# Two-layer graph attention on one core: layer 0's larger units scored and summed in two parts

## The chip, the cores and the metric

The kernel runs on one core of a Trainium2 chip. The metric is device time in microseconds from launch to end; lower is better. The engines are TensorE (PE, with its weight loads PEld), VectorE (DVE), ScalarE (ACT), GpSimd (POOL) and SyncE (SP); each works through its own queue in order and waits on semaphores for the others.

## The reference

Two graph attention layers over 8 batches of 2048 nodes with 256 channels, one adjacency matrix for all, each with a residual and a layer norm. Cut to layer 0, which the change touches:

```python
h1, h2, h3 = inp @ W1, inp @ W2, inp @ W3                 # per batch, 2048 x 256
e = leaky_relu(einsum('bnd,bmd->bnm', h1, h2), 0.2)
e = where(adj > 0, e, -1e12)
attention = softmax(e, axis=-1)
x = layernorm(x + relu(einsum('bnm,bmd->bnd', attention, h3)))
```

Layer 1 has four heads of 64 channels, logits that are sums of a source and a destination term, the same mask and softmax, elu, residual and layer norm. About one in 128 entries of adj is set, and the diagonal, so a node has some tens of neighbours at most.

## The kernel before

**Tiling.** The nodes are ranked by degree (in the setup) and cut into 16 tiles of 128 nodes. Tile t is given `SLOTS[t]` neighbour slots: 36, 24, 22, 21, 20, 19, 19, 18, 17, 17, 16, 15, 15, 14, 13, 12. A unit is one tile in one layer for one half h of the batches (four batches, `HB`). In layer 0 the units of half 0 run from t = 15 to t = 0, then those of half 1 in the same order; then 32 units of layer 1 follow. There are 298 slots in a half, so 596 in each layer.

**Gathering.** For each slot, POOL issues one indirect DMA (L196) that fetches, for each of the 128 nodes, the row of its k-th neighbour: 4 batches x 256 floats. Rows lie in `ring`, 16 buffers (`RING`) of two slots (`CHUNK`), 32 slots in all. A buffer is held from its gather until its last sum. In half 0 the neighbour lists of later tiles are made beside this (`neighbours`, L506 to L515), and their rows pass through the same ring.

**Scoring (`logits0`, DVE).** The product W1 W2^T is folded into the query: `u.g` (made in `before0` by transposing the tile's own rows and two projections). A slot takes four instructions (L568), one for each batch: a product of 128x256 with its sum as `e[:, b, k]`. When all slots of a part are scored, the softmax follows on a tile of 128 x 4 x K: leaky ReLU (L581), the mask's addition (L582), maximum (L586), subtraction (L587), exp on ACT (L588), sum (L591), reciprocal (L593) and scaling (L594).

**Summing (`sums0`).** For each slot ACT makes four diagonal matrices (L665, tile `dg`, four buffers, each of one slot) from the probabilities, and PE multiplies them with the slot's rows into two PSUM tiles of 128x512 (`acc`, L645, four buffers). The cut into 64x64 pieces spreads node halves over both tiles.

**After (`after0`).** The finished sums are copied to `hs` by ACT (L680), transposed on PE, projected with W3 (L427), and DVE adds the residual with the ReLU in it (L705) and takes the statistics (L384). ACT computes the inverse root from them (tile `z`, L395 and L396), normalises (L407), and PE transposes the result and makes layer 1's table rows (L729), which ACT copies (L737) and POOL stores.

**Parts.** A unit of more than 24 slots is scored and summed in two parts, each with a softmax of its own. That is t = 0 alone (18 + 18). At its end `shares` (L600 to L629) finds the common maximum of both parts, rescales, moves the factors to the nodes' places with eight PE records (L620) and two copies (L628); then ACT scales the first part (L686) and DVE adds the scaled second part (L689).

**Order.** The program is written out by a loop of ticks. Each tick belongs to one summed slot of the current unit. It issues gathers while ring buffers are free (`pump`), lets the scoring stream go on by up to two slots while `ahead`, the slots scored but not yet summed, is below a limit, and takes a step or two of the queues `starts` (`before0`), `ends` (`after0`) and `lists`. The limit is

```python
tick(left + units[min(j + 1, len(units) - 1)].K + LEAD)      # LEAD = 5
```

with `left` the slots of the unit still to be summed. A slot is scored at the earliest three ticks after its gather. POOL's instructions keep this order (`manual_schedule` for POOL); those of PE, DVE and ACT are ordered by the compiler, which takes the written order as priority.

Of the kernel before, what the change touches and what calls it, by code (L numbers as in the profile page):

```python
# [11 lines left out]
F32 = mybir.dt.float32  # L12
# [4 lines left out]
AF = mybir.ActivationFunctionType  # L17
ALU = mybir.AluOpType
# [18 lines left out]
SLOTS = (36, 24, 22, 21, 20, 19, 19, 18, 17, 17, 16, 15, 15, 14, 13, 12)  # L37
CHUNK = 2
RING = 16
LEAD = 5  # L40
LATE = 6

# [87 lines left out]
def fast_path(  # L130
# [27 lines left out]
    KC = C // P  # L158
    HB = B // 2
    HC = HB * C  # L160
    HG = HB * H
    HW = HC // 2
    CD = C + H
# [274 lines left out]
    class Unit:  # L438
        def __init__(self, layer, h, t):
            self.layer, self.h, self.t = layer, h, t  # L440
            self.K = SLOTS[t]
            self.name = f"{layer}_{h}_{t}"

            n = self.K if self.K <= RING * CHUNK * 3 // 4 else -(-self.K // 2)
            self.parts = [(k, min(n, self.K - k)) for k in range(0, self.K, n)]
            self.chunks = [[] for _ in self.parts]
            self.p = [None] * len(self.parts)
            self.ps = [None] * len(self.parts)

            self.m, self.s = [], []  # L450
            self.xo = None
            self.ready = False
# [99 lines left out]
    def logits0(u):  # L552

        while not u.ready:
            yield 0
        for i, (k0, K) in enumerate(u.parts):
            n, o = f"{u.name}_{i}", offs[u.t] + k0
            e = ep.tile([P, HB, K], F32, tag="e", name=f"e_{n}")
            for k in range(K):
                c, s = divmod(k, CHUNK)  # L560
                while len(u.chunks[i]) <= c:
                    yield 0
                while clock[0] < u.chunks[i][c][2] + 3:
                    yield 0
                rows = u.chunks[i][c][0]
                for b in range(HB):
                    jt = sp.tile([P, C], BF16, tag="j", name=f"j_{n}_{k}_{b}", bufs=4)
                    nc.vector.tensor_tensor_reduce(  # L568
                        out=jt,
                        in0=rows[:, s, ts(b, C)],  # L570
                        in1=u.g[:, ts(b, C)],
                        scale=1.0,
                        scalar=0.0,
                        op0=ALU.mult,
                        op1=ALU.add,
                        accum_out=e[:, b, k : k + 1],
                    )
                yield 1
            p = e
            wide = [P, HB, K]  # L580
            nc.vector.scalar_tensor_tensor(p, e, ALPHA, e, ALU.mult, ALU.max)  # L581
            nc.vector.tensor_tensor(  # L582
                p, p, neg[:, o : o + K].unsqueeze(1).to_broadcast(wide), ALU.add
            )
            m = sp.tile([P, HG], F32, tag="m1", name=f"m_{n}")[:, :HB]
            nc.vector.tensor_reduce(m, p, AX.X, ALU.max)  # L586
            nc.vector.tensor_tensor(p, p, m.unsqueeze(2).to_broadcast(wide), ALU.subtract)  # L587
            nc.scalar.activation(p, p, AF.Exp)  # L588
            yield 0
            sm = sp.tile([P, HG], F32, tag="s1", name=f"s_{n}")[:, :HB]  # L590
            nc.vector.tensor_reduce(sm, p, AX.X, ALU.add)  # L591
            if len(u.parts) == 1:
                nc.vector.reciprocal(sm, sm)  # L593
                nc.vector.tensor_tensor(p, p, sm.unsqueeze(2).to_broadcast(wide), ALU.mult)  # L594
            u.m.append(m)
            u.s.append(sm)
            u.p[i] = p
            yield 0

    def shares(u, G):  # L600


        f = sp.tile([P, 2, HG], F32, tag="f", name=f"f_{u.name}", bufs=1)[:, :, :G]
        top = sp.tile([P, HG], F32, tag="top", name=f"top_{u.name}", bufs=1)[:, :G]
        nc.vector.tensor_tensor(top, u.m[0], u.m[1], ALU.max)
        for i in range(2):
            nc.vector.tensor_tensor(f[:, i, :], u.m[i], top, ALU.subtract)
        nc.scalar.activation(f, f, AF.Exp)
        for i in range(2):
            nc.vector.tensor_tensor(u.s[i], u.s[i], f[:, i, :], ALU.mult)  # L610
        nc.vector.tensor_tensor(top, u.s[0], u.s[1], ALU.add)
        nc.vector.reciprocal(top, top)
        nc.vector.tensor_tensor(f, f, top.unsqueeze(1).to_broadcast([P, 2, G]), ALU.mult)
        fs = sp.tile([P, 2, 2, HG // 2], F32, tag="fs", name=f"fs_{u.name}", bufs=1)
        fs = fs[:, :, :, : G // 2]
        for r in range(2):
            rr = slice(64 * r, 64 * r + 64)
            pf = ps_tile(f"ps_f_{u.name}_{r}")[:, :G].rearrange("p (i g) -> p i g", i=2)
            for c in range(2):
                nc.tensor.matmul(  # L620
                    pf[64 * c : 64 * c + 64],
                    lhsT=ident[rr, rr],
                    rhs=f[rr, :, ts(c, G // 2)],
                    start=True,
                    stop=True,
                    tile_position=(64 * r, 64 * c),
                )
            nc.vector.tensor_copy(fs[:, :, r, :], pf)  # L628
        return fs  # L629
# [23 lines left out]

    def sums0(u):
        accs = []
        for i, (k0, K) in enumerate(u.parts):
            while u.p[i] is None:
                yield 0
            acc = [acc_tile(f"acc_{u.name}_{i}_{r}") for r in range(2)]
            for k in range(K):  # L660
                c, s = divmod(k, CHUNK)
                rows, n, _ = u.chunks[i][c]
                diag = dp.tile([P, HB, 64], F32, tag="dg", name=f"dg_{u.name}_{i}_{k}")
                for b in range(HB):
                    nc.scalar.activation(  # L665
                        diag[:, b, :], twice, AF.Copy, scale=u.p[i][:, b, k : k + 1]
                    )
                while evictions:
                    evictions.popleft()()
                add_slot(acc, k, K, rows[:, s, :], diag)  # L670
                if s == n - 1:
                    credits[0] += 1
                yield 1
            accs.append(acc)

        def evict():
            u.hs = hsp.tile([P, HC], F32, tag="hs", name=f"hs_{u.name}")
            if len(accs) == 1:
                for r in range(2):
                    nc.scalar.copy(u.hs[:, ts(r, HW)], accs[0][r])  # L680
                return
            fs = shares(u, HB)
            for r in range(2):
                for j in range(2):
                    v = u.hs[:, ts(2 * r + j, C)]
                    nc.scalar.activation(  # L686
                        v, accs[0][r][:, ts(j, C)], AF.Copy, scale=fs[:, 0, r, j : j + 1]
                    )
                    nc.vector.scalar_tensor_tensor(  # L689
                        v, accs[1][r][:, ts(j, C)], fs[:, 1, r, j : j + 1], v, ALU.mult, ALU.add  # L690
                    )

        evictions.append(evict)

# [266 lines left out]
    def tick(limit):  # L961
        pump()
        while late and late[0][0] <= clock[0]:
            late.popleft()[1]()
        for _ in range(2):
            if ahead[0] < limit:
                ahead[0] += next(stream, 0)
        for queue in queues:
            for _ in range(min(len(queue), 2)):
                if queue and next(queue[0], queue) is queue:  # L970
                    queue.popleft()
        clock[0] += 1
# [5 lines left out]
    for j, u in enumerate(units):  # L978
        begun = False
        if 0 < j and j + 2 < NT:  # L980
            lists.append(neighbours(up[j + 2]))
        if j == NT:
            ends.append(checks())
        while len(ends) > 1:
            tick(0)
        if 2 <= j < 10:
            b, i = divmod(j - 2, 2)
            n = ts(i, N // 2)

            nc.gpsimd.dma_start(xg[1][n, ts(b, C)], x[HB + b, n])  # L990
        if j + 3 < 2 * NT:

            own_rows(units[j + 3])
        left = float(u.K)
        for share in sums[u.layer](u):
            ahead[0] -= share
            left -= share
            tick(left + units[min(j + 1, len(units) - 1)].K + LEAD)
            if not begun and left <= u.K / 2 and j + 3 < len(units):
                begun = True  # L1000
                v = units[j + 3]
                starts.append(before[v.layer](v))
        ends.append(finish(u))
# [300 lines left out]
```

## Time and profile before

| | |
|---|---|
| time, median of 11 runs | 2482.49 us (2478.58 to 2498.56) |
| the profiled execution | 2483.11 us, its span 2481.3 us |
| mean granted TensorE clock | 0.868 |
| layer 0, first to last accumulating matmul | 150 to 1482 us |
| L568, scores, DVE | 2384 instructions, mean 421 ns |
| L665, diagonals, ACT | 2384 instructions, mean 339 ns |
| L645, layer 0's sums, PE | 9536 records, mean 410 ns |
| L196, layer 0's gathers, POOL | 596, mean 1052 ns |

In the profile, "idle before" is an engine's idle time just ahead of an instruction, and the arrow names what ended it. In a list of waits, the columns are the total in us, how often, and the longest. Scores are pipelined on DVE: one takes 421 ns, but they start some 345 ns apart.

### The profile page before, as it was taken

How to read it: one execution, taken by the hardware profiler on the slowest of the kernel's cores; microseconds unless marked ns; L12 is line 12 of the kernel's file. 1: busy time of each engine (PE TensorE's matmuls, PEld its weight loads, DVE VectorE, ACT ScalarE, POOL GpSimd, SP SyncE). 2: the span in 40 equal slices, each digit the busy share in tenths (PEclk: the TensorE clock that was granted, in tenths of full speed). 3: DMA queues.
4: the chain of work that ended last, by engine and by line, in shares of the span. 5: the costliest groups of instructions: out<-in, count | busy, mean ns of one | idle time of the engine just before them, and what ended most of it. 6: DMA issues, size and time to landing. Idle time of an engine off the chain costs nothing. (4 is left out here: it accounts for less than half of the span.)

```text
span 2481.3 us, 52177 instructions
## 1 busy us (share of the span) xinstructions
PE 1790.9 (72%) x16675; PEld 968.9 (39%) x16675; DVE 2004.3 (81%) x7073; ACT 1430.6 (58%) x4849; POOL 1518.8 (61%) x1486
## 2 busy tenths in 40 slices
PE   1157888788889778889898888666556667755664
PEld 0134556455555555656555543222212122222221
DVE  6699688888888666777878856988888798888996
ACT  6244566666666656767666674643455466543545
POOL 3374455565666445655556565777677777775773
PEclk9678989898989899999999998788778888886887
DMA  9797778798886668888888777997899999977992
GB/s 382 265 350 257 287 275 325 272 323 294 291 295 235 205 231 274 288 277 302 302 272 304 257 266 266 342 355 270 314 351 353 344 352 359 347 275 292 349 352 97
DMA packets 249419, 734.92 MB, mean 296 GB/s; under 512 B 63200, under 2 KB 72544, under 8 KB 246704
## 3 DMA queue, kind: packets, MB, share of 16 engines
q0 software_dynamic: 192512, 645.89, 72.8%
q1 hardware_dynamic: 55360, 84.44, 10.0%
q8 instruction: 135, 2.21, 0.4%
q10 hardware_dynamic: 1264, 1.18, 0.2%
q14 instruction: 148, 1.21, 0.1%
HBM read 708.35 MB, written 76.09 MB: 316 GB/s over the span
## 5 line engine op out<-in xcount | busy, mean ns | idle before, releaser
L568 DVE CUSTOM_DVE_ANT_0 j<-s,g 128x256 bf16<-128x256 f32 x2384 | 855.5, 421 | 209.7 <-DMA s<-xg,idx 199.5
L196 POOL DMA_INDIRECT s<-xg,idx x596 | 626.7, 1052 | 517.5 <-PE acc L645 302.1
L645 PE MATMUL acc<-s,ident 64*64 64x512 f32 x4768 | 611.3, 665 | 348.0 <-issue 293.3
L645 PE MATMUL acc<-s,dg 64*64 64x256 f32 x9536 | 696.8, 410 | 150.6 <-ACT dg L665 139.8
L196 POOL DMA_INDIRECT s<-qg,idx x596 | 606.0, 1017 | 234.7 <-issue 130.4
L665 ACT ACTIVATE dg<-twice,e 128x64 f32<-128x64 f32 x2384 | 616.7, 339 | 91.2 <-PE acc L645 88.2
L846 DVE TENSOR_TENSOR s<-s,p 128x2048 f32<-128x2048 f32 (+1 forms) x260 | 574.8, 2233 | 0.0
L645 PEld LDWEIGHTS acc<-s,dg 64*64 64x64 f32 x9536 | 375.4, 141 | 413.7 <-ACT dg L665 228.8
L645 PEld LDWEIGHTS acc<-s,ident 64*64 64x64 f32 x4768 | 211.0, 150 | 740.1 <-issue 592.6
L842 ACT ACTIVATE s<-s,e 128x64 f32<-128x64 f32 x1408 | 342.7, 334 | 45.7 <-DVE e L810 37.7
L395 ACT ACTIVATE z<-st,roots 128x4 f32<-128x4 f32 x64 | 19.1, 298 | 368.8 <-DVE st L384 368.8
L568 DVE DVE_READ_ACCUMULATOR2_ANT e<- 128x1 f32 x2384 | 195.2, 82 | 0.0
L204 POOL DMA_INDIRECT out_dram<-o,oidx x128 | 128.6, 1005 | 67.7 <-ACT o L407 31.6
L780 DVE TENSOR_TENSOR e<-s,own 128x32 f32<-128x32 f32 (+1 forms) x306 | 56.7, 189 | 123.2 <-DMA s<-qg,idx 121.6
L729 PE MATMUL ps_q<-wqs,x1T 128*128 128x264 f32 x512 | 136.9, 404 | 7.3 <-ACT x1T L419 4.8
L427 PE MATMUL ps_p_g<-A,xT 128*128 128x256 f32 x512 | 130.5, 400 | 3.3 <-ACT xT L419 3.3
L427 PE MATMUL ps_p_h<-w_sb,hT 128*128 128x256 f32 x512 | 128.8, 395 | 2.5 <-ACT hT L419 2.5
L729 PEld LDWEIGHTS ps_q<-wqs,x1T 128*128 128x128 f32 x512 | 97.0, 197 | 36.0 <-ACT x1T L419 7.5
L407 ACT ACTIVATE o<-xr,nmr,rstd 128x256 f32<-128x256 f32 x128 | 66.5, 589 | 76.2 <-DVE nmr L403 69.5
L427 PEld LDWEIGHTS ps_p_g<-A,xT 128*128 128x128 f32 x512 | 96.8, 197 | 33.5 <-ACT xT L419 8.8
L427 PEld LDWEIGHTS ps_p_h<-w_sb,hT 128*128 128x128 f32 x512 | 93.6, 192 | 38.2 <-issue 13.6
L588 ACT ACTIVATE e<-e 128x72 f32<-128x72 f32 (+11 forms) x34 | 8.8, 259 | 135.5 <-DVE e L587 135.3
(138 smaller groups left out, 1479.5 us busy)
## 6 DMA issues: line engine op xcount, KB each, us to landing
adj<-in_adj_dram SPq DMA_DIRECT2D x16, 1024.0 KB
xr<-xo SPq DMA_DIRECT2D x128, 128.0 KB
x1s<-y SPq DMA_DIRECT2D x32, 512.0 KB
xr<-x1s SPq DMA_DIRECT2D x32, 512.0 KB
s<-xg,idx POOLq DMA_INDIRECT x596
s<-qg,idx POOLq DMA_INDIRECT x596
edges<-adj SPq DMA_DIRECT2D x16, 512.0 KB
xg<-in_x_dram SPq DMA_DIRECT2D x4, 2048.0 KB
```

What stands on the lines that cost most here:

```text
L196: nc.gpsimd.indirect_dma_start(out=dst, out_offset=None, in_=table, in_offset=AT(ap=index, axis=0), bounds_check=table.shape[0] - 1, oob_i ...
L204: ins = nc.gpsimd.indirect_dma_start(out=table, out_offset=AT(ap=index, axis=0), in_=src, in_offset=None)
L395: nc.scalar.activation(z, var, AF.Ln, bias=w.roots[:, 0:1], scale=1.0 / C)
L407: nc.scalar.activation(dst[:, b, :], y[:, b, :], AF.Identity, bias=nmr[:, b : b + 1], scale=rstd[:, b : b + 1],)
L427: nc.tensor.matmul(pp[:, ts(j, C)], lhsT=srcT[:, ts((2 * i + j) * KC + k, P)], rhs=weight[:, k, :], start=(k == 0), stop=(k == KC - 1),)
L568: nc.vector.tensor_tensor_reduce(out=jt, in0=rows[:, s, ts(b, C)], in1=u.g[:, ts(b, C)], scale=1.0, scalar=0.0, op0=ALU.mult, op1=ALU.add, ...
L645: nc.tensor.matmul(out, lhsT=lhsT, rhs=rhs, start=(k == 0 and j == 0), stop=(k == K - 1 and (j == 1 or diag is None)), tile_position=(64 * ...
L665: nc.scalar.activation(diag[:, b, :], twice, AF.Copy, scale=u.p[i][:, b, k : k + 1])
L729: nc.tensor.matmul(pq[:, : C + 2 * H], lhsT=x1T[:, ts(i * KC + k, P)], rhs=w.sqs[:, k, j * H : j * H + CD + H], start=(k == 0), stop=(k == ...
L780: nc.vector.tensor_tensor(e[:, c * CHUNK : c * CHUNK + ns, :].rearrange("p s (b g) -> p s b g", b=HB), rows[:, :ns, :].rearrange("p s (b w ...
L842: nc.scalar.activation(v[:, a, g, :], v[:, a, g, :], AF.Copy, scale=pv[:, a, g : g + 1])
L846: nc.vector.tensor_tensor(v, v, pv.unsqueeze(3).to_broadcast([P, n * HB, H, D]), ALU.mult)
```

## The change

- Units of layer 0 with 16 slots or more (t = 0 to 10, in both halves) are cut in two parts. The first part has an even number of slots: 24 = 12 + 12, 22 = 12 + 10, 21 = 10 + 11, 20 = 10 + 10, 19 = 10 + 9, 18 = 10 + 8, 17 = 8 + 9, 16 = 8 + 8; 36 stays 18 + 18. Units of layer 1 are cut as before.
- Both parts lie in one score tile, `both`. The second part's softmax runs over one more column that holds the first part's maximum. After the exp this column is the factor by which the first part's weights shrink; multiplied with the first part's sum it goes into the common sum. The second part is fully normalised, and the same column, normalised, is the first part's factor.
- `spread_shares` moves this factor to the nodes' places (PE, then two ACT copies) as soon as the second softmax is done.
- At the fourth slot of the second part's sums ACT writes the scaled first part to `hs`; when the second part is summed, DVE adds it. `shares` remains for layer 1.
- The limit for scoring ahead counts parts in place of units: what is left of the part, the next part, and 5.
- The mask's addition is an operation of its own, as it was.

```diff
+SPLIT = 16
@@ Unit
-            n = self.K if self.K <= RING * CHUNK * 3 // 4 else -(-self.K // 2)
-            self.parts = [(k, min(n, self.K - k)) for k in range(0, self.K, n)]
+            n = self.K
+            if layer == 0 and n >= SPLIT:
+                n = CHUNK * ((n + 2) // (2 * CHUNK))
+            elif n > RING * CHUNK * 3 // 4:
+                n = -(-n // 2)
+            self.parts = [(0, n), (n, self.K - n)][: 1 if n == self.K else 2]
@@ logits0
-            e = ep.tile([P, HB, K], F32, tag="e", name=f"e_{n}")
+            last = i == len(u.parts) - 1
+            if i == 0:
+                both = ep.tile([P, 2, HB, MOST], F32, tag="e", name=f"e_{n}")
+            e = both[:, i, :, : 1 + K + 1]
...
+            v = p
+            if i:
+                v = e[:, :, : 1 + K]
+                nc.vector.tensor_copy(e[:, :, 0], u.m[0])
...
+            if i:
+                v = e[:, :, 1:]
+                nc.vector.tensor_tensor(e[:, :, 1 + K], e[:, :, 0], u.s[0], ALU.mult)
+            nc.vector.tensor_reduce(sm, v, AX.X, ALU.add)
+            if last:
                 nc.vector.reciprocal(sm, sm)
...
+                if i:
+                    u.fs = spread_shares(u, e)
...
+    def spread_shares(u, e):
+        fs = sp.tile([P, 2, 2], F32, tag="f0", name=f"f0_{u.name}", bufs=2)
+        for r in range(2):
+            rr = slice(64 * r, 64 * r + 64)
+            pf = ps_tile(f"ps_f0_{u.name}_{r}")[:, :2]
+            for c in range(2):
+                nc.tensor.matmul(
+                    pf[64 * c : 64 * c + 64],
+                    lhsT=ident[rr, rr],
+                    rhs=e[rr, ts(c, 2), 0],
+                    start=True,
+                    stop=True,
+                    tile_position=(64 * r, 64 * c),
+                )
+            nc.scalar.copy(fs[:, r, :], pf)
+        return fs
@@ sums0
+                if i == 1 and k == 3:
+                    u.hs = hsp.tile([P, HC], F32, tag="hs", name=f"hs_{u.name}")
+                    for r in range(2):
+                        for j in range(2):
+                            nc.scalar.activation(
+                                u.hs[:, ts(2 * r + j, C)], accs[0][r][:, ts(j, C)], AF.Copy,
+                                scale=u.fs[:, r, j : j + 1],
+                            )
...
         def evict():
+            if split:
+                for r in range(2):
+                    v = u.hs[:, ts(r, HW)]
+                    nc.vector.tensor_tensor(v, v, accs[1][r], ALU.add)
+                return
@@ the tick loop
+        ends_of = [u.K - k0 - K for k0, K in u.parts]
+        follow = [K for _, K in u.parts[1:]] + [units[min(j + 1, len(units) - 1)].parts[0][1]]
...
-            tick(left + units[min(j + 1, len(units) - 1)].K + LEAD)
+            i = next(i for i, end in enumerate(ends_of) if left > end or end == 0)
+            tick(left - ends_of[i] + follow[i] + LEAD)
```

More of the change, by code (lines that the diff above doesn't have):

```diff
@@ L160, in fast_path @@
     HC = HB * C
+    MOST = 2 + max(SPLIT - 1, SLOTS[0] // 2)
     HG = HB * H
@@ L575, in logits0 @@
                         op1=ALU.add,
-                        accum_out=e[:, b, k : k + 1],
+                        accum_out=e[:, b, 1 + k : 2 + k],
                     )
                 yield 1
-            p = e
-            wide = [P, HB, K]
-            nc.vector.scalar_tensor_tensor(p, e, ALPHA, e, ALU.mult, ALU.max)
+            p = e[:, :, 1 : 1 + K]
+            nc.vector.scalar_tensor_tensor(p, p, ALPHA, p, ALU.mult, ALU.max)
             nc.vector.tensor_tensor(
-                p, p, neg[:, o : o + K].unsqueeze(1).to_broadcast(wide), ALU.add
+                p, p, neg[:, o : o + K].unsqueeze(1).to_broadcast([P, HB, K]), ALU.add
             )
+            v = p
+            if i:
+                v = e[:, :, : 1 + K]
+                nc.vector.tensor_copy(e[:, :, 0], u.m[0])
             m = sp.tile([P, HG], F32, tag="m1", name=f"m_{n}")[:, :HB]
-            nc.vector.tensor_reduce(m, p, AX.X, ALU.max)
-            nc.vector.tensor_tensor(p, p, m.unsqueeze(2).to_broadcast(wide), ALU.subtract)
-            nc.scalar.activation(p, p, AF.Exp)
+            nc.vector.tensor_reduce(m, v, AX.X, ALU.max)
+            nc.vector.tensor_tensor(
+                v, v, m.unsqueeze(2).to_broadcast([P, HB, v.shape[2]]), ALU.subtract
+            )
+            nc.scalar.activation(v, v, AF.Exp)
             yield 0
             sm = sp.tile([P, HG], F32, tag="s1", name=f"s_{n}")[:, :HB]
-            nc.vector.tensor_reduce(sm, p, AX.X, ALU.add)
-            if len(u.parts) == 1:
-                nc.vector.reciprocal(sm, sm)
-                nc.vector.tensor_tensor(p, p, sm.unsqueeze(2).to_broadcast(wide), ALU.mult)
+            v = p
+            if i:
[3 more added lines that the diff above has]
+            if last:
+                nc.vector.reciprocal(sm, sm)
+                v = p if i == 0 else e[:, :, : 1 + K]
+                nc.vector.tensor_tensor(
+                    v, v, sm.unsqueeze(2).to_broadcast([P, HB, v.shape[2]]), ALU.mult
+                )
+                if i:
+                    u.fs = spread_shares(u, e)
             u.m.append(m)
@@ L598, in logits0 @@
             yield 0
+    def spread_shares(u, e):
[11 more added lines that the diff above has]
+                    tile_position=(64 * r, 64 * c),
+                )
+            nc.scalar.copy(fs[:, r, :], pf)
+        return fs
     def shares(u, G):
@@ L655, in sums0 @@
         accs = []
+        split = len(u.parts) == 2
         for i, (k0, K) in enumerate(u.parts):
@@ L672, in sums0 @@
                     credits[0] += 1
+                if i == 1 and k == 3:
[5 more added lines that the diff above has]
+                                scale=u.fs[:, r, j : j + 1],
+                            )
                 yield 1
@@ L676, in evict @@
         def evict():
-            u.hs = hsp.tile([P, HC], F32, tag="hs", name=f"hs_{u.name}")
[L678 to L682, printed above, removed]
-            for r in range(2):
[L684 to L691, printed above, removed]
+            if split:
[3 more added lines that the diff above has]
+                return
+            u.hs = hsp.tile([P, HC], F32, tag="hs", name=f"hs_{u.name}")
+            for r in range(2):
+                nc.scalar.copy(u.hs[:, ts(r, HW)], accs[0][r])
         evictions.append(evict)
```

## The prediction, made before the changed kernel was run

> **What bounds the kernel now.** I read the busy totals first, then busy time by stretch, then the waits of each stretch, then the timeline of one unit, then the groups by shape.
>
> ```profile
> PE 1790.9 (72%) x16675; PEld 968.9 (39%) x16675; DVE 2004.3 (81%) x7073; ACT 1430.6 (58%) x4849; POOL 1518.8 (61%) x1486
> ```
>
> No engine is full over the span, so one has to go by stage. Layer 0 sums its slots from 150 to 1482 us. Two stretches of it hold the units that the change splits anew, t = 10 to 2, nine in each half (bounds: the ends of the units' last accumulating matmuls). Columns: busy time (and instructions) of PE, PEld, DVE, ACT, POOL, then granted clock, DMA share and GB/s.
>
> ```profile
> 334.80:720.50 385.70, 329.53 (x3392) 216.01 (x3392) 326.46 (x1778) 249.59 (x875) 220.40 (x211) 0.92 0.86 301
> 1016.70:1375.70 359.00, 323.70 (x3366) 209.08 (x3364) 280.77 (x1496) 246.56 (x862) 203.76 (x197) 0.96 0.86 294
> ```
>
> Call them A (half 0, neighbour lists are still being made on DVE) and B (half 1). PE is idle 56.2 us in A and 35.3 in B; DVE 59.2 and 78.2. PE is the fuller one, nearly level with DVE in A. Who is PE waiting for? First A, then B:
>
> ```profile
> ACT z L395 <- DVE st L384: 65.1, 9, 10.9
> POOL s L196 <- PE acc L645: 56.5, 29, 7.0
> PE acc L645 <- ACT dg L665: 54.8, 14, 7.1
> DVE j L568 <- DMA s<-xg,idx: 50.2, 37, 4.8
> ```
>
> ```profile
> POOL s L196 <- PE acc L645: 104.7, 58, 5.9
> DVE j L568 <- DMA s<-xg,idx: 70.3, 48, 5.1
> ACT z L395 <- DVE st L384: 44.0, 9, 7.2
> PE acc L645 <- ACT dg L665: 34.1, 15, 5.2
> ```
>
> Nearly all of PE's idle time (54.8 of 56.2; 34.1 of 35.3) ends with a diagonal from ACT, and ACT sits nine times in nine units at z, waiting for statistics from DVE. One unit of A, ACT and then PE:
>
> ```profile
> 429.01 1.06 ACT L665 ACTIVATE dg<-twice,e 128x64 f32<-128x64 f32 x4 [1.79 <-PE acc L645]
> 440.95 0.30 ACT L395 ACTIVATE z<-st,roots 128x4 f32<-128x4 f32 x1 [10.88 <-DVE st L384]
> ```
>
> ```profile
> 430.73 3.68 PE L645 MATMUL acc<-s,dg 64*64 64x256 f32 x64
> 441.55 5.20 PE L645 MATMUL acc<-s,dg 64*64 64x256 f32 x48 [7.13 <-ACT dg L665]
> ```
>
> ACT stands 10.88 us at z, so no diagonals are made; PE uses up those it has and then stands 7.13 us. So it is a ring of waits: DVE's statistics lie in its queue behind scored slots; those wait for landings (DVE's only large wait); the gathers wait for PE to free ring buffers; PE waits for ACT, ACT for DVE. PE never waits for a softmax itself: in these units the last score of a unit, counted off in the trace, ends 10 to 29 us before its first sum.
>
> **The change, part by part.** Mask: before adds it by an operation of its own too (L582), so this part is worth nothing.
>
> *Order.* This is the part with the gain. Counted in the trace of before, 33 to 36 slots past the unit's end are scored before its second statistics, in all eighteen units, and diagonals for 8 to 10 slots are made before z. The tick loop followed on paper gives nearly the same (31 to 36; 10 or 11), since the ring of 32 slots is the limit there, not `left + next K + 5`. With the new limit, `rest of the part + next part + 5`, the loop on paper puts 23 to 29 slots there: about 9 fewer. A slot costs DVE four scores started 0.345 us apart (the timeline), 1.38 us; nine are 12.4 us, more than any wait at z. So stretches could close up to the busier engine plus what is added.
>
> *DVE, per newly split unit.* Small operations take 0.16 us on 4 elements (L397) and about 0.23 on 72; at 40 elements I take 0.19. Unsplit, 18 slots: seven operations, 1.54 us. Split: 5 x 0.19, then 5 x 0.19 + copy 0.16 + product 0.16 + reciprocal 0.17 + last product 0.19, together 2.58: 1.0 more (0.8 to 1.2 with 0.16 or 0.23 for each). Eviction moves from ACT to DVE: two 128x512 additions reading PSUM, nearest row L892, 0.686 us: 1.37. Sum 2.4 us, for 20 units 48 us. It lies in DVE's idle 59.2 (A) and 78.2 (B); without that cover it is the slow rival below.
>
> *ACT.* Rows:
>
> ```profile
> L680 ACT COPY hs<-acc 128x512 f32<-128x512 f32 x60 | 31.8, 584 | 6.1 <-PE acc L645 6.1
> L686 ACT ACTIVATE hs<-acc,fs 128x256 f32<-128x256 f32 x8 | 3.1, 475 | 4.2 <-DVE fs L628 4.2
> ```
>
> Minus two copies (1.17), plus four scalings (1.90), one more exp (0.26), two tiny copies from PSUM (not in the trace; between nothing beyond their neighbour and 0.38 like L737; taken 0.29 like L396, 0.58 together): +1.6 us a unit. ACT is idle 136 us in A, 112 in B; covered, unless it falls where PE lives on its four diagonals.
>
> *PE.* Eight more matmul records of two columns a unit; L620's eight fill about 0.4 us with their weight loads: 9 us for 22 units, added to PE's floor.
>
> *New waits.* DVE is now waited for at three more places in a unit: transposes of hs (T) behind its eviction, PE's share matmuls behind the second softmax, ACT's second exp. Behind the share matmuls in PE's queue stand the following sums; behind ACT's share copies the next diagonals. Priced at the share matmuls: from the unit's end DVE has eviction 1.37, four slots 5.5, softmax 2.6, together 9.5 us; PE has till there four slots at 1.09, two transposes at 0.66 and a projection of 2.0, 7.7 us: 1.8 us of idle, and 0 if the compiler places them later (DVE, ACT and PE orders are its choice, only POOL's is kept as written: in the trace statistics stand up to 2.5 slots off the source's order in A and B, and 13 off at the last unit of half 0). I take 1.0 x 20 = 20 us; ends 0 and 36 us. The single hs buffer, now taken at slot 3 of part 1, was read out in the first slots of part 0, and the sums of part 0 are long done then: nothing. POOL issues the same gathers in the same order; the first part is even, so chunks stay as many.
>
> *The 36-slot units.* They were split already. Of the waits, PE stood 9.87 us at 836.48 and 4.63 at 1486.58 behind L686, which waited for L628 at the end of a chain of small DVE operations. Shares are now ready early and only the addition is left: 14.5 less about 4.5, a gain of 10.
>
> *Layer 1.* Its parts stay, its limit changes only beside the 36-slot unit, where the ring binds first: 0.
>
> **The sum.** A can fall to DVE's 326.5 + 9 x 2.4 = 348, a gain of at most 37.6; B to PE's 323.7 + 9 x 0.4 = 327, at most 31.7; the t = 11 units (idle 5.1 and 4.2, lead falls from 33 to 21) 9. t = 1 keeps its lead of 36 on paper: 0. Together 78, of which I take 60%, 47, because a DVE with idle time will be given later slots and drift back towards the ring's end. So 47 + 10 - 20 = 37 off. The profiled execution took 2483.11 us (span 2481.3 and 1.8 around it), 0.6 above the median of 11: 2446.
>
> A rule that speaks against this: Trainium skill, Perfetto Trace Analysis, Optimizing Scalar/DVE Operations, gives each DVE operation a fixed part, about 60 ns on SBUF and 125 on PSUM against ScalarE's 51 on PSUM, and advises larger operations on a saturated engine. By it (an estimate, with 1.03 ns an element from the rows above) seven more small operations and two PSUM additions of 512 cost 1.7 us a unit, 35 us in all, instead of the rows' 48, and the forecast would not move, for the cover is larger than both. The rows agree with its direction: L680 0.584 on ACT, L892 0.686 on DVE.
>
> **Rivals.**
>
> *DVE pays (slower), 0.34.* Place: A above all, where 50.2 of DVE's 59.2 idle us are landings: busy plus ring wait is the whole time. If the compiler fills DVE with later slots up to the ring's end, statistics stand behind 33 slots as before, and 2.4 us a unit go on top: 48, less 10 for the 36-slot units: 2521. It decides if the landing wait stays above some 5.5 us a unit in A. For: those 13 slots. Against: in A hardly any DVE time is free to be filled.
>
> *Handed back (no change), 0.14.* PE's wait at z goes, but share matmuls, eviction and second exp take it: 47 + 10 against 20 x 2.8: 2482.
>
> *Everything closes up, 0.10.* 78 + 10 off, no new wait: 2395. Against: PE and DVE would both have to run almost without a gap.
>
> **Numbers.** Forecast 0.42, 2446, its own range 2415 to 2472. What can be told from no change is about 0.3% (7.5 us). Faster: 0.42 + 0.10 and a little of the third, 0.53; within 0.3%: 0.12; slower: 0.35. The range for 8 in 10 reaches from 2405, where only the tail of "closes up" is left out, to 2505, half way up the slow case.
>
> **What would show it.** Right: z's wait for statistics in A and B falls from 109.1 us to below 50, landing waits fall from 120.5 with it, PE's idle time per unit falls to 2 to 4 us, no PE wait near 9.87 after the first 36-slot unit. Wrong: statistics still stand behind 33 scored slots; or PE waits for the share matmuls' DVE operations or for DVE's addition by more than 2 us a unit; or A's DVE shows the same landing waits and more busy time.

## The result and the profile after

The changed kernel takes 2592.26 us (median of 8 runs, 2583.7 to 2597.48), the kernel before 2485.24 beside it: a ratio of 1.0427, interval [1.0408, 1.0446]. It is 107 us slower where 37 us faster was forecast, outside the range. All of it lies in layer 0: its last sum ends at 1587.8 us in place of 1481.9, and what follows takes 991.8 in place of 999.5.

The page's busy totals of the changed kernel, then busy time in the same nine units of each half (A and B, cut at the ends of the same units' last sums, so the stretches are longer now):

```profile
PE 1812.4 (70%) x16835; PEld 974.7 (38%) x16835; DVE 2041.9 (79%) x7237; ACT 1445.4 (56%) x4951; POOL 1518.3 (59%) x1486
```

```profile
333.90:760.50 426.60, 341.70 (x3446) 214.75 (x3444) 340.47 (x1845) 253.43 (x912) 219.69 (x212) 0.91 0.79 273
1066.80:1474.00 407.20, 337.36 (x3438) 212.82 (x3442) 299.29 (x1583) 257.34 (x923) 205.14 (x196) 0.93 0.76 260
```

A is 40.9 us longer than before (426.6 to 385.7), B 48.2 (407.2 to 359.0). PE's idle time (stretch less its busy time) went from 56.2 to 84.9 and from 35.3 to 69.8. The waits of A, then of B:

```profile
POOL s L199 <- PE acc L687: 100.5, 32, 7.2
DVE j L578 <- DMA s<-xg,idx: 72.6, 49, 4.7
ACT e L603 <- DVE e L600: 69.7, 15, 9.5
PE ps_t_h L420 <- DVE hs L731: 52.3, 8, 10.1
...
PE acc L687 <- ACT dg L708: 21.2, 20, 3.4
...
ACT z L398 <- DVE st L387: 18.0, 8, 4.6
```

```profile
POOL s L199 <- PE acc L687: 134.6, 43, 9.1
DVE j L578 <- DMA s<-xg,idx: 95.5, 60, 4.0
ACT e L603 <- DVE e L600: 58.4, 15, 8.5
...
PE ps_t_h L420 <- DVE hs L731: 28.1, 6, 6.2
...
PE acc L687 <- ACT dg L708: 22.2, 21, 3.3
ACT z L398 <- DVE st L387: 21.4, 9, 4.5
```

The waits that the prediction named did fall: ACT at z from 109.1 us to 39.4, PE at the diagonals from 88.9 to 43.4. (Below 50 at z was the prediction's sign of being right. It is no sign of a gain: ACT's wait at the exps, the second one among them, rose from 48.3 us to 128.1 in A and B.) PE now stands at the transposes of hs, for DVE's addition of the two parts (L731), and DVE waits more for landings, 168.1 us in place of 120.5. One such place in A, PE first, then DVE:

```profile
657.42 1.96 PE L687 MATMUL acc<-s,dg 64*64 64x256 f32 x32
669.43 1.11 PE L420 MATMUL ps_t_h<-ident,hs 128*128 128x128 f32 x4 [10.06 <-DVE hs L731]
```

```profile
660.91 0.43 DVE L578 CUSTOM_DVE_ANT_0 j<-s,g 128x256 bf16<-128x256 f32 x1 [1.04 <-DMA s<-xg,idx]
...
662.30 0.36 DVE L520 MAX8 m<-some 128x8 f32<-128x192 f32 x1
...
668.35 0.42 DVE L578 CUSTOM_DVE_ANT_0 j<-s,g 128x256 bf16<-128x256 f32 x1
668.69 1.28 DVE L731 TENSOR_TENSOR hs<-hs,acc 128x512 f32<-128x512 f32 x2
```

PE has summed its last slot at 659.4 and stands 10.06 us. DVE stands only 1.04 us of this, for a landing: it scores slots of later units and makes a neighbour list, and only then comes to the addition, which takes 1.28 us. The price of the addition is its place in DVE's queue, not its length. Counted in the trace as for the statistics before, in the 18 units of A and B 26.5 to 29 slots past the unit's end are scored ahead of it, where the written order has 13 to 17. The second statistics too stand behind 33 to 36 slots, as they did before the change, and not behind 23 to 29.

### The profile page after: what moved, and what is told of

Same layout as the page of the kernel before. It is cut to its first block, busy times and chain, and to the rows that moved or that the text cites. A ratio compares the mean times of both kernels' runs of the same rounds, so it can differ in the third digit from the quotient of the medians.

```text
span 2579.6 us, 52772 instructions
## 1 busy us (share of the span) xinstructions
PE 1812.4 (70%) x16835; PEld 974.7 (38%) x16835; DVE 2041.9 (79%) x7237; ACT 1445.4 (56%) x4951; POOL 1518.3 (59%) x1486
## 5 line engine op out<-in xcount | busy, mean ns | idle before, releaser
L687 PEld LDWEIGHTS acc<-s,dg 64*64 64x64 f32 x9536 | 369.3, 141 | 354.5 <-ACT dg L708 174.3
L773 PE MATMUL ps_q<-wqs,x1T 128*128 128x264 f32 x512 | 143.1, 420 | 23.2 <-ACT x1T L422 15.1
L420 PE MATMUL ps_t_h<-ident,hs 128*128 128x128 f32 x256 | 57.5, 366 | 143.8 <-DVE hs L731 107.8
L603 ACT ACTIVATE e<-e 128x40 f32<-128x40 f32 (+9 forms) x54 | 13.0, 241 | 214.2 <-DVE e L600 214.2
```

The costliest lines, as they stand in the source:

```text
L420: nc.tensor.transpose(pt[:, ts(j, P)], src[:, ts(4 * i + j, P)], ident)
L687: nc.tensor.matmul(out, lhsT=lhsT, rhs=rhs, start=(k == 0 and j == 0), stop=(k == K - 1 and (j == 1 or diag is None)), tile_position=(64 * ...
L773: nc.tensor.matmul(pq[:, : C + 2 * H], lhsT=x1T[:, ts(i * KC + k, P)], rhs=w.sqs[:, k, j * H : j * H + CD + H], start=(k == 0), stop=(k == ...
```

## Experiments

Two theories at first. E: the addition on DVE stands behind slots that the compiler has drawn forward, and PE waits for it. W: the added work itself (second softmax, second exp, share matmuls) is the loss. "Of before" below is the ratio to the kernel before, run beside it on the same chip.

**e1, DVE's order held as written.** The compiler may no longer reorder DVE:

```diff
-    ctx.enter_context(tc.manual_schedule(engines={mybir.EngineType.Pool}))
+    ctx.enter_context(
+        tc.manual_schedule(engines={mybir.EngineType.Pool, mybir.EngineType.DVE})
+    )
```

> The changed kernel with DVE's instructions kept in the written order. Theory E (the eviction on DVE stands behind 27 to 29 scored slots that wait for landings, and PE's transposes wait for it): it now stands behind about 15, PE's waits for it fall from 107.8 us to below 30, and the time to 2440 to 2500. Rival W (the added work on DVE and the second softmax of a unit are the loss): the time stays above 2560, since no work is taken away.

Measured: 2711.58 us, 1.0921 of before [1.0878, 1.0964]. Theory E's range is missed; the time is above 2560, as rival W had it, but the trace shows another reason than W's. Layer 0's last sum ends at 1500.0 (1587.8 in the changed kernel); what follows takes 1207.6 instead of 991.8, and one wait there, 46.7 us in the changed kernel, is now by far the largest of PE's (waits from 1501 us on):

```profile
PE acc L689 <- DVE s L892: 428.5, 168, 9.2
```

So in layer 0 the held order brings back 88 us: the additions of A and B stand behind 13 to 17 slots, as on paper, and PE's wait for them falls from 107.8 us to 4.7. In layer 1 the written order of DVE is much worse than the compiler's.

**e2, the parts are added on PE**, ahead of the last slot, and ACT copies hs:

```diff
+                if i == 1 and k == K - 1:
+                    for r in range(2):
+                        nc.tensor.matmul(
+                            acc[r], lhsT=ident, rhs=u.hs[:, ts(r, HW)], start=False, stop=False
+                        )
...
-                    v = u.hs[:, ts(r, HW)]
-                    nc.vector.tensor_tensor(v, v, accs[1][r], ALU.add)
...
+                nc.scalar.copy(u.hs[:, ts(r, HW)], accs[-1][r])
```

> The changed kernel with the addition of both parts made on PE, before the last slot (two full 128x512 matmuls with the identity, about 2 us a unit, 43 us of PE in all), and the eviction copied by ACT as before. Theory E: PE's waits for hs from DVE are gone, 100 us come back and some 40 are paid: 2500 to 2540. Rival W: only 1.4 us a unit leave DVE, and PE has 43 more: 2570 to 2630.

Measured: 2545.25 us, 1.0241 [1.0204, 1.0278]; 47 less than the changed kernel, just past the upper end that E gave. What is paid on PE can be read from its group of instructions:

```profile
L715 PE MATMUL acc<-hs,ident 128*128 128x512 f32 x88 | 42.6, 606 | 0.0
```

**e3, the kernel before with eviction on DVE** (only `nc.scalar.copy` to `nc.vector.tensor_copy` for the 30 unsplit units):

> The kernel before with one part of the change alone: the 30 unsplit units are evicted by two DVE copies in place of two ACT copies. Theory E: 4 to 6 us a unit of PE waiting for hs, 2570 to 2640. Rival W: 1.3 us of DVE a unit, 2490 to 2525.

Measured: 2543.53 us, 1.0233 [1.0196, 1.0270]: 61 us slower, between the two expectations, 2.0 us for a unit that has 1.3 us of added DVE work. The trace shows the same wait without any split:

```profile
PE ps_t_h L417 <- DVE hs L680: 90.8, 24, 10.3
```

So the wait comes with the move to DVE, without any split, but E had its price too high. Part of it is given back: PE's wait for the diagonals fell from 139.8 us before to 108.2.

**e4, the limit of before** in the changed kernel (`left + next K + LEAD`):

> The changed kernel with the limit of before for scoring ahead (rest of the unit + next unit + 5). Theory E: the compiler fills DVE with later slots anyway, so next to nothing changes: 2580 to 2605, statistics behind 33 to 36 slots. Rival L (the shorter limit starves the second part): 2480 to 2540.

Measured: 2620.58 us, 1.0552 [1.0514, 1.0591]. Both miss. The second statistics stand behind 33 to 36 slots under either limit, as E said, and yet the old limit is 28 us slower. So the new limit is a gain of the change, but not through the place of the statistics, where the prediction had it. Through which, the trace does not settle: PE now stands 55.4 us at the share matmuls for DVE's softmax (5.9 in the changed kernel), but only 50.4 for the addition (107.8).

**e5, DVE's order held in layer 0 alone.** The guard of e1 around the ticks of layer 0:

```diff
+    held = tc.manual_schedule(engines={mybir.EngineType.Pool, mybir.EngineType.DVE})
+    held.__enter__()
...
+        if j == 2 * NT:
+            held.__exit__(None, None, None)
```

> The changed kernel with DVE's order held as written in layer 0 alone (in the first experiment it was held in layer 1 too). Theory O (in layer 0 the order that the compiler gives DVE is the loss, in layer 1 the written order is): layer 0 as in the first experiment, last sum at about 1500 us, layer 1 as in the changed kernel, 992 us after it: 2480 to 2515. Rival W (added work): above 2560.

Measured: 2502.62 us, 1.0085 [1.0065, 1.0106], inside the range of theory O. 90 us of the 107 come back with no work taken away, so W alone can't be the cause. Two of the waits of stretch A in this kernel (322.1 to 717.4 us):

```profile
PE ps_f L631 <- DVE e L614: 35.6, 8, 7.1
...
DVE hs L731 <- PE acc L687: 22.3, 7, 4.9
```

Now DVE waits at the addition for PE, not PE for DVE. ACT's wait at z is gone from the longest waits, as are the landings. What PE waits for instead are the share matmuls, the place that the prediction priced: 77.4 us over 16 places in layer 0.

**e6, as e5 with the share matmuls late:**

```diff
-                if i:
-                    u.fs = spread_shares(u, e)
+                if i:
+                    u.both = e
...
+                if i == 1 and k == 1:
+                    u.fs = spread_shares(u, u.both)
```

> As e5, with the share matmuls issued at the second slot of the second part's sums and not right behind the second softmax. Theory S (what is left in e5 is PE waiting at the share matmuls for DVE's softmax, 77 us in the first experiment): those waits go, 2425 to 2470. Rival: the same lateness of DVE shows at the eviction or at the diagonals instead, and the time stays within 15 us of e5.

Measured: 2469.59 us, 0.9943 [0.9920, 0.9966]: 33 us less than e5, at the upper end of theory S, and 15 us less than the kernel before. This is the version that beats both. Part of the rival holds too: PE's wait for the diagonals in layer 0 rose from 73.6 us in e5 to 125.2. A and B take 389.6 and 365.2 us here, no less than before (385.7 and 359.0): against the kernel before, the gain lies in the other units. In B:

```profile
DVE hs L733 <- PE acc L687: 43.1, 8, 7.6
PE acc L687 <- ACT dg L708: 34.3, 22, 4.1
...
ACT z L398 <- DVE st L387: 25.7, 7, 6.2
```

One unit of A, DVE and then ACT:

```profile
665.44 1.28 DVE L733 TENSOR_TENSOR hs<-hs,acc 128x512 f32<-128x512 f32 x2 [4.76 <-PE acc L687]
```

```profile
691.24 0.30 ACT L398 ACTIVATE z<-st,roots 128x4 f32<-128x4 f32 x1 [8.21 <-DVE st L387]
```

DVE stands 4.76 us at the addition until PE has its last sum, then works without a gap up to the statistics, and ACT stands 8.21 us at z.

**e7, the control: the kernel before with DVE's order held in layer 0.**

> The kernel before with DVE's order held as written in layer 0, the control of e5. Theory O: its written order and its compiled one are nearly the same (31 to 36 scored slots ahead of the statistics in both), so 2465 to 2500. Rival (holding the order helps or hurts by itself): off by more than 20 us.

Measured: 2499.25 us, 1.0060 [1.0037, 1.0083], inside the range. Holding the order costs 15 us by itself, so e5 and e6 have to be set against this: with DVE's order held, the change costs 3 us, which is within the intervals, and with the shares late it gains 30. A and B take 410.8 and 371.1 us in e7 (328.2 to 739.0 and 1021.8 to 1392.9), so against this control most of e6's gain, 21.2 and 5.9 us, does lie in the units split anew.

**e8, `SPLIT = 25`:** only the 36-slot units have two parts, in the new way.

> The changed kernel with the threshold at 25 slots: only the 36-slot units have two parts, as before the change, but in its new way, shares ready early and the addition on DVE. Theory of the prediction (the chain of shares at the end of these two units cost 14.5 us of PE): 2468 to 2480. Theory E (the addition on DVE waits behind scored slots): a gain of less than 5, 2478 to 2490.

Measured: 2486.67 us, 0.9998 [0.9979, 1.0017]: no gain, as E has it. The 10 us of the prediction are not there. After the first 36-slot unit PE stood 9.87 us behind the chain of shares before the change; in this kernel it is the addition:

```profile
848.24 1.97 PE L420 MATMUL ps_t_h<-ident,hs 128*128 128x128 f32 x8 [9.62 <-DVE hs L731]
```

**e9 to e11.** e9 lets ACT copy the second part's sums to hs and adds nothing, so the first part's sums are left out:

```diff
-                    v = u.hs[:, ts(r, HW)]
-                    nc.vector.tensor_tensor(v, v, accs[1][r], ALU.add)
+                    nc.scalar.copy(u.hs[:, ts(r, HW)], accs[1][r])
```

> The changed kernel, compiler's order, with the second part's sums alone copied to hs by ACT, so that the first part's sums are left out and nothing is added on DVE or PE. It prices the addition on DVE without the PE work of the second experiment. Theory E: 75 to 100 us below the changed kernel, 2490 to 2515. Rival W (shares, second softmax and second exp carry at least half of the loss): 2530 to 2560.

e10 is e6 with `LEAD = 9`:

> As e6 with LEAD 9 in place of 5: four more slots scored ahead of the eviction, 19 to 21 in place of 15 to 17. In e6 DVE waits 89 us at the eviction for PE's sums, so it comes too early there. Theory: that wait falls below 50 and the time to 2440 to 2464. Rival: DVE has slack to spare and PE waits for ACT at the diagonals whatever DVE does: within 7 us of e6.

e11 is the changed kernel with e6's late shares, in the compiler's order:

> The changed kernel, compiler's order, with only the share matmuls moved to the second slot of the second part's sums. In the changed kernel PE hardly waits for them (3.1 us at the most in a unit), so Theory E gives within 15 us of the changed kernel, 2577 to 2605. Rival S (they are a main part of the loss in this order too): below 2565.

These three ran on a chip on which the kernel before takes 2645.1 us, so their times can't be held against the expected ones, and ratios only with care (e12 below). Ratios: e9 1.0129 [1.0081, 1.0177], e10 0.9939 [0.9917, 0.9961], e11 1.0265 [1.0218, 1.0312]. e10 against e6's 0.9943 is no difference, although the additions of A and B now stand behind 17 to 21 slots, four more, and DVE's wait at the addition hardly moves (84.9 us for 89.0): the theory fails, and the rival's number holds. e9 and e11 are below the changed kernel's 1.0427, but by how much was open without that kernel on the same chip. Hence four more.

**e12 to e15, a two by two.** e12 is the changed kernel, e13 is e9, e14 is e11, e15 has both edits.

> The changed kernel once more, as the corner of a two by two with the three runs beside it on one chip: addition on DVE or not, share matmuls early or late. 1.038 to 1.047 of the kernel before.

> As e9 (first part's sums left out, ACT copies the second part's to hs, nothing added on DVE), beside the changed kernel on the same chip. Theory E: at least 60 us less than the changed kernel. Rival W: less than 50 less.

> As e11 (share matmuls late, all else as changed), beside the changed kernel on the same chip. If e11's 1.0265 was the change and not that chip: 30 to 45 us less than the changed kernel. If it was the chip: within 15 us of it.

> Both: first part's sums left out with ACT copying to hs, and the share matmuls late. What stays above the kernel before is the rest of the change (second softmax and exp, four scalings, shares). If the two costs add up, the gains of e13 and e14 add: 0 to 20 us above the kernel before. If they are one lateness of DVE that shows at either place: no more than 10 us less than the better of e13 and e14.

They too fell on a chip where the kernel before takes longer, 2629.35 us, but all corners are there:

| | early shares | late shares |
|---|---|---|
| addition on DVE | 2703.42, 1.0275 [1.0229, 1.0320] | 2692.11, 1.0225 [1.0163, 1.0286] |
| first part left out, ACT copies | 2657.93, 1.0105 [1.0053, 1.0158] | 2648.84, 1.0076 [1.0049, 1.0103] |

On this chip the changed kernel is 74 us slower than before, less than the 1.038 expected. The addition on DVE is worth 45.5 of them. By the bounds on record that is rival W's case (less than 50) and not theory E's (at least 60), but it is still the larger part of the 74. The late shares are worth 11.3, which the intervals do not tell from nothing; by e14's expectation, e11's lower ratio came from its chip. Together the two bring 54.6, where the two alone add up to 56.8, as if they were two costs; but 54.6 is also only 9.1 more than the better one alone, as if they were one. The bounds of both theories are met, so this is not settled. What stays, 19.5 us, is at the upper end of what was expected.

## Why the prediction was wrong

**What bounds the kernel: right.** PE waits for ACT, ACT at z for DVE, DVE for landings, POOL for PE.

**That nine slots fewer would close the stretches up (the 47 us of the sum): borne out in part at most.** In e1 and e5 the second statistics stand behind 23 to 29 slots, and z waits no more than 1.8 us in any of the 18 units, but there PE stands at the share matmuls. In e6 the statistics stand just where they do in e5 and that wait is gone, and z waits up to 8.2 us again (69.3 us in A and B, 109.1 before) and PE 81.5 us at the diagonals (88.9 before). Against the control e7, where DVE's order is held too, A and B gain 27.1 us; against the kernel before, none. What e6 has in place of the rest is DVE's wait at the addition for PE's sums, 70.2 us in A and B, a wait the sum had nowhere. That this is what keeps the statistics late was not tried by itself.

**The step that failed first: "With the new limit ... the loop on paper puts 23 to 29 slots there".** The loop on paper was right to the slot, as e1 shows; DVE does not run it. Where DVE's order was left to it, the compiler drew later slots forward up to the ring's end, 33 to 36 again. The prediction knew this (statistics stood 13 slots off at one place), took 40% off a gain for it, and gave the rest to the chance that "in A hardly any DVE time is free to be filled". These runs read as if DVE's agreement with the paper order in the trace of before came from the ring's limit (33 to 36 slots there, 31 to 36 with the order held in e7), not from the compiler keeping to it; why it draws slots forward was not tried.

**The step that cost most: the eviction's move to DVE, priced at 1.37 us of work.** Its work was priced well (1.28 us) and its wait not at all. The prediction took the new wait at the share matmuls (1.8 us a unit) as the price of all three places. With the slots drawn forward, the addition stands behind 26.5 to 29 of them, and PE behind the addition: 107.8 us of waiting over 20 places in the whole trace, 80.4 of it in the 18 units of A and B. The prediction had this among its signs of being wrong (more than 2 us a unit), but no cost for it in the sum. On the chip of the two by two its removal brings 45.5 of 74 us; on a chip of the first kind e2 brings 47 of 107 net, with 42.6 us of PE paid for it.

**The share matmuls: within the ends ("0 and 36 us") in the written order, where they cost 33 us (e5 to e6).** In the compiler's order PE waits 5.9 us there for the second softmax, and issuing them late brings 11.3 us, no more than the intervals.

**Sizes.** DVE's added work is 1.8 us a unit, (340.5 - 326.5 + 299.3 - 280.8) / 18, not 2.4. PE's is 1.4 (from 329.5 and 323.7 to 341.7 and 337.4), not 0.4. Over the whole trace PE's busy time grew by 21.5 us, 13.0 of it in the transposes of hs (44.5 before, 57.5 after); why these records run longer was not tried. ACT's is 0.8, not 1.6. None of these makes the difference. **The 36-slot units** gained nothing (e8): the chain of small operations that was removed gave its 9.87 us to the addition, 9.62.

**The rivals.** "DVE pays" had the mechanism, slots up to the ring's end and landing waits that stay, and came out at 2521, 71 us short, because it priced the added work and not the eviction's place in the queue. "Handed back" had the eviction among the places that take the gain, at 2.8 us a unit for all of them; PE's waits for the addition alone are 5.4 us each. The rule of the Trainium skill (Perfetto Trace Analysis, Optimizing Scalar/DVE Operations: a higher fixed part on PSUM for DVE than for ScalarE) points to the right side (a copy of 128x512 took 681 ns on DVE in e3, 584 on ACT before). But the 0.15 us for two evictions, an estimate from its figures, is small beside the 2.0 us a unit that e3 measured.

**Open.** Why the change costs 107 us on one kind of chip and 74 on another was not tried; the traces show that PE's wait for the addition is 107.8 us in the first and 65.9 in the second (e12). Nor was what the rest of 19.5 us is made of.

## What to carry to other kernels

Be wary of moving an operation that another engine waits for to the engine that runs furthest ahead: look at how many instructions stand ahead of it in that queue, and what those wait for, before asking how long it takes. If the compiler orders an engine, a limit in the written program is only a wish on that engine's idle time; before building on it, find a place in the trace where the limit binds, and see whether it was kept. Holding the order of one engine in one stage is a cheap test of such a theory, with the kernel before held in the same way as its control.

## What had not been expected

Holding DVE's written order costs 15 us in layer 0 of the kernel before (e7), but some 209 us in layer 1 of the changed one (1207.6 in e1 to 998.7 in e5 from layer 0's last sum to the end). And chips differ: the kernel before takes 2482 to 2485 us on some and 2629 and 2645 on two others, with a higher granted clock there (the changed kernel 0.885 in e12, 0.868 in its first profile). For the changed kernel most of the difference is in layer 1: in e9 to e15 1083 to 1100 us follow layer 0's last sum, in place of 992 to 1001 in the traces of the first kind of chip. So times don't carry over, and even the changed kernel's ratio went from 1.0427 to 1.0275.
